# Five kinds of small instruction of the last layers on VectorE in place of GpSimd, with another tie seed

## The chip, the cores and the metric

The kernel runs on one core of a Trainium2 chip. Its engines work side by side, each through its own instruction stream in order: TensorE (PE in the profile; PEld is its weight load), VectorE (DVE), ScalarE (ACT), GpSimd (POOL) and SyncE (SP, which issues nearly all DMAs). An instruction waits for semaphores that other engines raise, and whatever stands behind it on its engine waits with it. The metric is the device time of one execution in microseconds, lower is better. Before the change it is 1130.74 us (median of three runs, 1130.67 to 1131.31).

## The reference: what is computed

The input x is 32 sequences of 64 tokens with 256 features, and a context of the same shape goes with it. Four layers run one after the other, all in float32:

```
x = L0(x, ctx)   # cross attention, 8 heads of 64, over the feature axis; residual
x = L1(x, ctx)   # cross attention, 16 heads of 16; keys and values from LayerNorm(ctx);
                 # x + tanh(gate) * out
x = L2(ctx, x)   # x as latents: attention of x over [ctx, x], RMSNorm, MLP 256-1024-256 with gelu,
                 # plus x
x = L3(x, ctx)   # h = x + selfattention(LayerNorm(x)); h = h + crossattention(LayerNorm(h), ctx);
                 # h + MLP(LayerNorm(h)), 256-1024-256 with gelu
```

In L3 the scores are `scores * mask - 10000 * (1 - mask)` before the softmax. LayerNorm is `(x - mean) * rsqrt(var + 1e-5) * scale + bias`; the kernel folds its scale into the rows of the weight matrix that follows, and its bias into that product's bias.

## The kernel before

Tokens are handled in 8 groups of 256 (two tiles of 128 tokens). Precision comes from splitting: a float32 operand v of a large product is written as a rounded high part hi and a low part v - hi, and three products (hi with hi, hi with low, low with hi) are summed in PSUM. So every weight matrix, every token matrix that is projected and every attention output needs a rounded copy (on ACT) and a subtraction (on VectorE or GpSimd).

L0 is written straight into the engines' streams, in the order of the code, with the first weights' preparation filled in between. It runs to about 459 us. Its instructions carry line 156 in the profile.

L1 to L3 make one plan. The work is cut into 80 attention sets: 16 for L1 (sets 0 to 15), 32 for L2 (16 to 47), 16 for L3's self attention (48 to 63) and 16 for its cross attention (64 to 79). A set covers 128 tokens and all heads (half the heads in L2). Its chain is: scores on PE into the PSUM tile s; in L3 a product with the mask on VectorE (`E<-s,m` for self attention, `E<-s,mk` for cross attention) and an addition on GpSimd (`E<-E,c` or `E<-E,ck`); maximum on VectorE (`mx`); subtraction on VectorE (in L1 and L2 straight from PSUM, `E<-s,mx`), in L3 in every other set on GpSimd (`E<-E,mx` in both cases); Exp on ACT; sum and reciprocal on VectorE (`sm`); in L1 and L2 the scaling by the reciprocals on GpSimd (`E<-E,sm`); transposes on PE, copied by ACT (`PTe`); product with the values on PE. In L3 the output is scaled in place of E (`rb`, VectorE). It is split into `xTho` (ACT) and `xTlo` (a subtraction, in L1 and L2 on VectorE from PSUM, in L3 on GpSimd); `a_fin`, lines 1089 to 1105, does this. There are three E tiles and one tile s, so two to three sets are under way at once.

Around the sets lie "steps": for each group the norm, the split of the context, the projections to keys, values and queries, the output projection and the MLP. Each has a due time, counted in sets. A norm (`norm_steps`, line 1197) has three steps. `ln_stats` (line 888) takes mean and variance with bn_stats and bn_aggr on VectorE, and its factor through `rsqrt` (line 750): epsilon is added (tile `rsq`), then GpSimd raises the result to the power -0.5 (`rstda`; `rstdm` for the norm before the MLP). `ln_apply` (line 899) makes minus mean times factor (`nmra`, `nmrm`), and ACT normalises with the two as bias and scale. `turn` transposes. Its parameter `load` is true for the norms of L1 alone, whose input is the loaded context; there are 16 norms of L3's attentions and 8 before its MLP. `ctx_steps` (line 1229) loads and splits the context for L2 and L3 (`xTh`, `xTl`). `load_unit` (line 503) loads a weight, multiplies its rows by the norm's scale where there is one (tile `wraw`, or `boot` where a spare buffer takes its place) and splits it. In the planned part the 8 such weights are those of L3: keys, values and queries of the self attention, the queries of the cross attention, and the four parts of the first MLP matrix.

The plan then decides the order. `Plan.cost` gives each instruction a duration by engine, form and width, and `Plan.order` is a list scheduler: again and again it takes, among the engines' ready instructions, the one that can start first, and where several can, the one with the smallest due time. To each due time a random number between 0 and TIE sets is added, drawn from SEED. The engine of an instruction and its modelled cost thus decide where it and all others stand, and the seed does as well. What comes out is written into the five streams; on the chip each stream runs in exactly that order, waiting where it must. All planned instructions carry line 125 in the profile, so they are told apart by their tiles. SyncE's DMAs are in the plan, too.

```python
getattr(self.engines[o.key], o.method)(*[real(x) for x in o.p], **{k: real(x) for k, x in o.k.items()})   # 125
at.urgent = at.due + ties.uniform(0, self.TIE) - (3.0 if ... else 0.0)
t, at = min(((t, at) for t, at in cand if t <= t0), key=lambda x: (x[1].urgent, x[1].index))
```

Of the kernel before, what the change touches and what calls it, by code (L numbers as in the profile page):

```python
# [93 lines left out]
class Plan:  # L94
# [2 lines left out]


    RING = {"pj": 40}
    SEED, TIE = 4, 0.5  # L100

    def __init__(self, engines):
        self.engines = engines
# [305 lines left out]
def mk_kernel(ctx: ExitStack, tc: tile.TileContext, a: dict, out: bass.AP):  # L409
# [93 lines left out]
    def load_unit(w, key, slot, ap, rows=None, mul=None, biases=(), then=None):  # L503

        cur["rawn"] += 1
        if cur["raws"] == 2 or cur["rawn"] % 2:
            raw = plan.tile(wraw, "r", [P, 2, D], F32, "wraw", nm("wraw"), 2)
        else:
            raw = wraws[cur["rawn"] // 2 % (cur["raws"] - 2)]
        SY.dma_start(raw, ap.rearrange("(k p) n -> p k n", p=P))  # L510
        yield
        for fn in biases:
            fn(raw)
        t = plan.tile(wpool if slot < NW else cur["w"], "ww", [P, 2, 2, D], F32R, f"w{slot}", nm("w"), 1)
        if rows is not None:
            for k in range(2):
                G.tensor_scalar(raw[:, k], raw[:, k], rows[:, k:k + 1], None, ALU.mult)
        elif mul is not None:
            G.tensor_scalar(raw, raw, mul, None, ALU.mult)
        A.copy(t[:, 0], raw)  # L520
        (V if slot < 4 and plan.on else G).tensor_tensor(t[:, 1], raw, f32(t[:, 0]), ALU.subtract)
        w[key] = (t[:, 0], t[:, 1])
        if then:
            then()
        yield
# [221 lines left out]
            SY.dma_start(m3[i * 64:(i + 1) * 64], a["mask3"])  # L747
        V.tensor_scalar(c3, m3, -1.0, 10000.0, ALU.add, ALU.mult)

    def rsqrt(dst, var, n, eps):  # L750
        t = plan.tile(small, "s", [P, n], F32, "rsq", nm("rsq"), 3)
        G.tensor_scalar(t, var, eps, None, ALU.add)
        G.tensor_tensor(dst, t, nhalf[:, 0:n], ALU.pow)


# [129 lines left out]
            return lambda: V.scalar_tensor_tensor(x1, av[:, 0:D], cst0, s["xt"], ALU.add, ALU.add)  # L885


    def ln_stats(x, tag):

        st = wt([P, 2, 6], F32, "st" + tag, 2)  # L890
        mv = wt([P, 2, 2], F32, "mv" + tag, 2)
        for i in range(2):
            V.bn_stats(st[:, i], x[:, i])
            V.bn_aggr(mv[:, i], st[:, i])
        rstd = wt([P, 2], F32, "rstd" + tag, 2)
        rsqrt(rstd, mv[:, :, 1], 2, 1e-5)
        return mv, rstd

    def ln_apply(x, mv, rstd, tag):
        z = wt([P, 2, D], F32, "z", 2)  # L900
        nmr = wt([P, 2], F32, "nmr" + tag, 2)
        for i in range(2):
            G.tensor_scalar(nmr[:, i:i + 1], mv[:, i, 0:1], rstd[:, i:i + 1], -1.0, ALU.mult, ALU.mult)
            A.activation(z[:, i], x[:, i], AF.Identity, bias=nmr[:, i:i + 1], scale=rstd[:, i:i + 1])
        return z

# [182 lines left out]
    def a_fin(u):  # L1089
        st, i = u["st"], u["i"]  # L1090
        if i == 0 and u["s"] == 0:
            st["o"] = fm_tiles("o")
        o_ = u["at"]
        c = slice(u["s"], u["s"] + 1) if u["two"] else slice(0, 2)
        hv, lv = [t[:, c, i * P:(i + 1) * P] for t in st["o"]]
        ov = o_[:, 0:D].rearrange("p (c t) -> p c t", c=2)[:, c]
        if u["kind"] == "k":
            A.copy(hv, ov)
            V.tensor_tensor(lv, ov, f32(hv), ALU.subtract)
        else:  # L1100
            rb = wt([P, 2, P], F32, "rb", 2)
            A.copy(rb.rearrange("p c t -> p (c t)"), o_[:, D:2 * D])
            V.tensor_tensor(rb, ov, rb, ALU.mult)
            A.copy(hv, rb)
            G.tensor_tensor(lv, rb, f32(hv), ALU.subtract)

    def out_add(w, x, resid, dst):

# [88 lines left out]
    def norm_steps(l, g, key, load, due, src=()):  # L1197

        st = grp.setdefault((l, g), {})
        n = f"{key}{l}{g}"  # L1200

        def fetch():
            st["raw"] = wt([P, 2, D], F32, "craw", 1)
            SY.dma_start(st["raw"], ctok[g])
        x = (lambda: st["raw"]) if load else (lambda: xs[g])
        if load:
            step(n + "a", due - 3, fetch, *src)

        def stats():
            st["ln"] = ln_stats(x(), key)  # L1210

        def apply():
            st["z"] = ln_apply(x(), *st["ln"], key)

        def turn():
            st[key] = to_fm(st["z"], rg if rg == "n" else "")
        rg = "n" if key == "m" else "x"
        step(n + "b", due - 2, stats, *((n + "a",) if load else src))
        step(n + "c", due - 1, apply, n + "b")
        step(n, due, turn, n + "c")  # L1220
# [8 lines left out]
    def ctx_steps(l, g, due, src=()):  # L1229
        st = grp[l, g]  # L1230
        n = f"c{l}{g}"

        def fetch():
            st["raw"] = wt([P, 2, D], F32, "craw", 1)
            SY.dma_start(st["raw"], a["ctxT"][:, g * D:(g + 1) * D].rearrange("(k p) t -> p k t", p=P))

        def split_():
            hi, lo = fm_tiles()
            A.copy(hi, st["raw"])
            G.tensor_tensor(lo, st["raw"], f32(hi), ALU.subtract)  # L1240
            st["c"] = (hi, lo)
        step(n + "a", due - 2, fetch, *src)
        step(n, due, split_, n + "a")
# [431 lines left out]
```

## Time and profile before

| | us |
|---|---|
| median of three runs | 1130.74 |
| profiled execution, its own time | 1132.07 |
| its span, first to last instruction | 1130.3 |
| PE busy | 1067.8 (94%) |
| VectorE busy | 894.9 (79%) |
| ACT busy | 906.3 (80%) |
| GpSimd busy | 761.8 (67%) |
| planned part, about | 459 to 1130 |
| sets 48 to 79 (L3's attentions) begin on VectorE | 785.9 to 1056 |

The times of stretches come from one profiled execution, 1.33 us over the median. A row of a group of instructions names the engine, the operation, the tiles written and read, the shapes and the count, then the busy time, the mean duration, and the idle time of the engine just before such instructions with what ended it. Matmul ends are modelled and matmuls overlap, so a busy PE can have room. The 40 digits of a slice view stand for 28.3 us each.

The rows of the instructions that the change touches, as the whole profile groups them (those with `boot` as output and a scale as second input are the row scales in the spare buffer):

```
L125 POOL TENSOR_TENSOR xTlo<-rb,xTho 128x256 fp32r<-128x256 f32 x32 | 29.0, 906
L125 POOL TENSOR_TENSOR xTl<-boot,xTh 128x512 fp32r<-128x512 f32 x16 | 22.4, 1403
L125 POOL TENSOR_SCALAR wraw<-wraw,vecs 128x256 f32<-128x256 f32 x18 | 16.5, 925
L125 POOL TENSOR_SCALAR nmra<-mva,rstda 128x1 f32<-128x1 f32 x48 | 12.5, 272
```

They hold L1's and L2's instructions as well, which stay where they are.

### The profile page before, as it was taken

To read this page: it belongs to the slowest core of one execution; us is meant where nothing else is said; L and a number is where in the kernel's file an instruction comes from. 1 tells how busy PE (TensorE), PEld (TensorE's weight loads), DVE (VectorE), ACT (ScalarE), POOL (GpSimd) and SP (SyncE) were. 2 spreads that over 40 slices of the span, in tenths; PEclk is the share of its full clock that TensorE was granted. 3 is DMA by queue.
4 is the path that set the end of the run, shared out by engine and by line. 5 is a ranking of instruction groups with operands and counts; after the bars stand their busy time and mean duration, and the time that the engine had idled before them with its cause. 6 is when DMAs were issued, how large, how long until landed. Compare 5 with 4: busy or idle time off the path is not lost.

```text
span 1130.3 us, 35569 instructions
## 1 busy us (share of the span) xinstructions
PE 1067.8 (94%) x14396; PEld 872.2 (77%) x14396; DVE 894.9 (79%) x1575; ACT 906.3 (80%) x2326; POOL 761.8 (67%) x829
## 2 busy tenths in 40 slices
PE   6999999999999999899999999999999988889998
PEld 4666666666666666788898989998988877779998
DVE  4889989897888777688888878777878878777842
ACT  2888888887888789577778889889898777888974
POOL 3788888886778667635546634477866989996520
PEclk9999999999999999899999999999999989989999
DMA  3001211111110100311211100000000111110000
GB/s 96 21 25 36 61 35 49 35 34 44 34 34 25 34 16 2 93 37 58 68 47 47 34 26 26 21 29 22 21 20 21 49 51 51 43 34 21 11 20 29
DMA packets 41300, 41.21 MB, mean 36 GB/s; under 512 B 7059, under 2 KB 37796, under 8 KB 41136
## 3 DMA queue, kind: packets, MB, share of 16 engines
q1 hardware_dynamic: 40816, 38.54, 10.9%
q8 instruction: 114, 1.87, 0.7%
q10 hardware_dynamic: 320, 0.40, 0.1%
q14 instruction: 50, 0.41, 0.1%
HBM read 26.30 MB, written 2.10 MB: 25 GB/s over the span
## 4 chain that ended last, share of the span: by engine, by line
PE 59%; DVE 15%; ACT 10%; POOL 10%; issue 4%; DMA 0%; SPq 0%; DVEq 0%; POOLq 0%; ACTq 0%
PE pj L125 39%; PE pt L156 6%; ACT E L156 5%; PE av L156 5%; PE sc L156 4%; PE s L125 4%; DVE mx L156 3%; POOL E L125 3%; DVE E L125 2%; DVE PT L156 2%; ACT PT L156 2%; DVE sB L156 2%; POOL E L156 2%; DVE mx L125 2%; PE pt L125 1%
## 5 line engine op out<-in xcount | busy, mean ns | idle before, releaser
L156 POOL TENSOR_TENSOR E<-E,rs 128x512 f32<-128x512 f32 x256 | 263.5, 1040 | 84.0 <-DVE rs L156 64.5
L156 ACT ACTIVATE E<-sc,mx 128x256 f32<-128x256 f32 x512 | 238.4, 481 | 23.2 <-DVE rs L156 21.9
L156 DVE TENSOR_REDUCE mx<-sc 128x4 f32<-128x1024 f32 x128 | 155.8, 1217 | 2.8 <-PE sc L156 1.4
L156 PE MATMUL sc<-cd,T 64*128 64x256 f32 x1024 | 144.0, 400 | 10.5 <-ACT E L156 10.0
L125 POOL TENSOR_TENSOR E<-E,sm 128x512 f32<-128x512 f32 x96 | 101.1, 1078 | 68.9 <-DVE sm L125 56.1
L156 PE MATMUL av<-PT,us 128*64 128x256 f32 x1024 | 125.0, 385 | 0.0
L156 PEld LDWEIGHTS pt<-ident,E 64*128 64x128 f32 x2048 | 83.6, 139 | 43.6 <-POOL E L156 15.8
L156 PEld LDWEIGHTS av<-PT,us 128*64 128x64 f32 x1024 | 68.3, 136 | 54.7 <-issue 20.4
L156 PEld LDWEIGHTS sc<-cd,T 64*128 64x128 f32 x1024 | 89.6, 189 | 25.8 <-ACT E L156 17.8
L125 DVE TENSOR_REDUCE sm<-E 128x16 f32<-128x1024 f32 (+1 forms) x80 | 96.0, 1200 | 15.3 <-ACT E L125 15.3
L156 ACT ACTIVATION_READ_ACCUMULATOR E<-sc,mx 128x1 f32 x512 | 108.0, 211 | 0.0
L156 PE MATMUL pt<-ident,E 64*128 64x64 f32 x2048 | 98.2, 228 | 6.1 <-ACT PT L156 2.2
L125 ACT COPY PTe<-pj 128x512 f32<-128x512 f32 x160 | 88.0, 590 | 19.2 <-PE pj L125 17.1
L125 PE MATMUL pj<-ident,E 128*128 128x128 f32 x640 | 90.8, 281 | 8.0 <-DVE rb L125 2.5
L156 ACT COPY PT<-pt 128x512 f32<-128x512 f32 x128 | 75.6, 591 | 24.3 <-PE pt L156 22.8
L125 PE MATMUL pj<-w,xThh 128*128 128x256 f32 x512 | 93.4, 287 | 0.1
L125 PE MATMUL pj<-xThn,w 128*128 128x256 f32 x512 | 92.2, 285 | 0.7 <-DVE rb L125 0.4
L156 DVE COPY PT<-pt 128x512 f32<-128x512 f32 x128 | 86.0, 672 | 5.2 <-PE pt L156 5.1
L125 ACT ACTIVATE E<-E 128x1024 f32<-128x1024 f32 x80 | 84.9, 1062 | 5.8 <-DVE E L125 4.6
L125 PEld LDWEIGHTS pj<-ident,E 128*128 128x128 f32 x640 | 71.6, 143 | 16.7 <-issue 3.6
L125 DVE TENSOR_TENSOR xTlh<-u,xThh 128x512 fp32r<-128x512 f32 x64 | 54.8, 861 | 29.9 <-ACT xThh L125 29.5
L156 DVE RECIPROCAL rs<-sm 128x2 f32<-128x2 f32 x256 | 40.1, 156 | 46.5 <-ACT E L156 43.7
(223 smaller groups left out, 2798.3 us busy)
## 6 DMA issues: line engine op xcount, KB each, us to landing
kb<-kfm SPq DMA_DIRECT2D x44, 128.0 KB
xd<-in_x SPq DMA_DIRECT2D x32, 128.0 KB
cd<-in_ctx SPq DMA_DIRECT2D x32, 128.0 KB
boot<-in_ctxT SPq DMA_DIRECT2D x16, 256.0 KB
kb<-kfm SPq DMA_DIRECT2D x64, 64.0 KB
xt<-in_x SPq DMA_DIRECT2D x16, 128.0 KB
boot<-in_ctx SPq DMA_DIRECT2D x8, 256.0 KB
out<-x SPq DMA_DIRECT2D x8, 256.0 KB
```

The lines of the kernel that those rows point to most:

```text
L125: getattr(self.engines[o.key], o.method)(*[real(x) for x in o.p], **{k: real(x) for k, x in o.k.items()})
L156: return f(*p, **k)
```

## The change

In L3 five kinds of instruction go to VectorE: the addition of epsilon in the norms, minus mean times factor (one instruction for the pair of tiles in place of two), the row scales of the weights that the plan loads, the low part of the context (L3 alone, `l == 3`), and the low part of the attention output where the tile index i is 0, every other set. The power stays on GpSimd. The seed of the ties goes from 4 to 9; with that, and with the other engines and costs, the scheduler puts the whole planned part into a new order. L0 and the first weights are as before.

```diff
@@ -97,7 +97,7 @@
 
 
     RING = {"pj": 40}
-    SEED, TIE = 4, 0.5
+    SEED, TIE = 9, 0.5
 
     def __init__(self, engines):
         self.engines = engines
@@ -514,7 +514,7 @@
         t = plan.tile(wpool if slot < NW else cur["w"], "ww", [P, 2, 2, D], F32R, f"w{slot}", nm("w"), 1)
         if rows is not None:
             for k in range(2):
-                G.tensor_scalar(raw[:, k], raw[:, k], rows[:, k:k + 1], None, ALU.mult)
+                (V if plan.on else G).tensor_scalar(raw[:, k], raw[:, k], rows[:, k:k + 1], None, ALU.mult)
         elif mul is not None:
             G.tensor_scalar(raw, raw, mul, None, ALU.mult)
         A.copy(t[:, 0], raw)
@@ -747,9 +747,9 @@
             SY.dma_start(m3[i * 64:(i + 1) * 64], a["mask3"])
         V.tensor_scalar(c3, m3, -1.0, 10000.0, ALU.add, ALU.mult)
 
-    def rsqrt(dst, var, n, eps):
+    def rsqrt(dst, var, n, eps, late=False):
         t = plan.tile(small, "s", [P, n], F32, "rsq", nm("rsq"), 3)
-        G.tensor_scalar(t, var, eps, None, ALU.add)
+        (V if late else G).tensor_scalar(t, var, eps, None, ALU.add)
         G.tensor_tensor(dst, t, nhalf[:, 0:n], ALU.pow)
 
 
@@ -885,7 +885,7 @@
             return lambda: V.scalar_tensor_tensor(x1, av[:, 0:D], cst0, s["xt"], ALU.add, ALU.add)
 
 
-    def ln_stats(x, tag):
+    def ln_stats(x, tag, late):
 
         st = wt([P, 2, 6], F32, "st" + tag, 2)
         mv = wt([P, 2, 2], F32, "mv" + tag, 2)
@@ -893,14 +893,17 @@
             V.bn_stats(st[:, i], x[:, i])
             V.bn_aggr(mv[:, i], st[:, i])
         rstd = wt([P, 2], F32, "rstd" + tag, 2)
-        rsqrt(rstd, mv[:, :, 1], 2, 1e-5)
+        rsqrt(rstd, mv[:, :, 1], 2, 1e-5, late)
         return mv, rstd
 
-    def ln_apply(x, mv, rstd, tag):
+    def ln_apply(x, mv, rstd, tag, late):
         z = wt([P, 2, D], F32, "z", 2)
         nmr = wt([P, 2], F32, "nmr" + tag, 2)
+        if late:
+            V.scalar_tensor_tensor(nmr, mv[:, :, 0], -1.0, rstd, ALU.mult, ALU.mult)
         for i in range(2):
-            G.tensor_scalar(nmr[:, i:i + 1], mv[:, i, 0:1], rstd[:, i:i + 1], -1.0, ALU.mult, ALU.mult)
+            if not late:
+                G.tensor_scalar(nmr[:, i:i + 1], mv[:, i, 0:1], rstd[:, i:i + 1], -1.0, ALU.mult, ALU.mult)
             A.activation(z[:, i], x[:, i], AF.Identity, bias=nmr[:, i:i + 1], scale=rstd[:, i:i + 1])
         return z
 
@@ -1102,7 +1105,7 @@
             A.copy(rb.rearrange("p c t -> p (c t)"), o_[:, D:2 * D])
             V.tensor_tensor(rb, ov, rb, ALU.mult)
             A.copy(hv, rb)
-            G.tensor_tensor(lv, rb, f32(hv), ALU.subtract)
+            (G if i else V).tensor_tensor(lv, rb, f32(hv), ALU.subtract)
 
     def out_add(w, x, resid, dst):
 
@@ -1207,10 +1210,10 @@
             step(n + "a", due - 3, fetch, *src)
 
         def stats():
-            st["ln"] = ln_stats(x(), key)
+            st["ln"] = ln_stats(x(), key, not load)
 
         def apply():
-            st["z"] = ln_apply(x(), *st["ln"], key)
+            st["z"] = ln_apply(x(), *st["ln"], key, not load)
 
         def turn():
             st[key] = to_fm(st["z"], rg if rg == "n" else "")
@@ -1237,7 +1240,7 @@
         def split_():
             hi, lo = fm_tiles()
             A.copy(hi, st["raw"])
-            G.tensor_tensor(lo, st["raw"], f32(hi), ALU.subtract)
+            (V if l == 3 else G).tensor_tensor(lo, st["raw"], f32(hi), ALU.subtract)
             st["c"] = (hi, lo)
         step(n + "a", due - 2, fetch, *src)
         step(n, due, split_, n + "a")
```

## The prediction

> **What bounds the kernel now.** I read the page's slices first, to see where the limit changes; then busy time by stretch, cut where the last part's attention sets begin; then the groups, waits and timeline inside the tight stretch.
>
> ```profile
> PE   6999999999999999899999999999999988889998
> POOL 3788888886778667635546634477866989996520
> PEclk9999999999999999899999999999999989989999
> ```
>
> TensorE (PE) is full nearly everywhere, except in slices 33 to 36 of 40 (about 904 to 1017 us), where GpSimd (POOL) shows nines and the granted clock dips twice. The next view cuts 858 to 1130 us where VectorE (DVE) takes up sets 56, 60, 64, 68, 72, 76 and where the last set, 79, has begun (sets 48 to 79 are the last part's).
>
> ```profile
> core 0: us, PE busy (x) PEld busy (x) DVE busy (x) ACT busy (x) POOL busy (x), PEclk, DMA share, GB/s
> 858.00:883.90 25.90, 24.09 (x405) 21.04 (x403) 21.98 (x33) 22.06 (x45) 18.66 (x15) 1.00 0.06 21
> 883.90:916.60 32.70, 30.90 (x427) 27.62 (x426) 24.99 (x47) 21.73 (x48) 29.65 (x28) 0.84 0.16 51
> 916.60:949.30 32.70, 27.35 (x418) 24.05 (x418) 28.81 (x47) 26.77 (x57) 31.82 (x31) 0.95 0.20 61
> 949.30:976.90 27.60, 24.36 (x380) 21.41 (x379) 23.85 (x37) 23.39 (x50) 26.60 (x27) 1.00 0.11 36
> 976.90:1030.20 53.30, 47.66 (x606) 43.73 (x607) 37.67 (x52) 44.66 (x90) 48.93 (x53) 0.94 0.11 34
> 1030.20:1056.00 25.80, 25.80 (x350) 24.30 (x350) 21.83 (x32) 22.84 (x42) 15.71 (x12) 1.00 0.04 13
> ```
>
> From 883.9 to 1030.2 (146.3 us, sets 60 to 75) GpSimd is busy 137.0 us, 94%, and VectorE 115.3, 79%. PE's busy share there flatters it: back to back, a 128x256 matmul starts 0.119 us after the last one, a 128x128 transpose 0.109, a set's 16 score groups take 0.70 (gaps and lengths in PE's records), and by these prices sets 60 to 75 hold only 95.6 us of matmuls and 11.2 of scores: PE has some 40 us to spare. GpSimd sets the pace, and the waits of this stretch agree (total, times, longest):
>
> ```profile
> DVE mx L125 <- POOL E L125: 8.3, 5, 2.9
> PE pj L125 <- POOL xTl L125: 4.5, 3, 2.2
> ```
>
> The first line: VectorE's maximum waits for GpSimd's mask addition; the second: PE waits for the context's low part, one of the moved instructions.
>
> **The change, part by part.** Five kinds of instruction leave GpSimd.
>
> - Epsilon added to the variance (rsq): 23 seen, 7.1 us.
> - Minus mean times factor (nmr): 46 of [128,1], 13.6 us; on VectorE one of [128,2] for a pair.
> - Row scales of 8 weights (wraw, boot): 16 of 128x256, 15.8 us.
> - The context's low part (xTl): 8 of 128x512, 11.7 us.
> - The output's low part (xTlo), every other set: 16 at 0.906, 14.5 us.
>
> Together 63 us. In the tight stretch the rows sum to 38 us: rsq 3.6, nmr 7.1, scales 8.3, xTl 11.7, half of xTlo 7.5. GpSimd falls from 137 to about 100 of 146 us and no longer sets the pace.
>
> What VectorE takes on. In the new program's order, 51 moved instructions lie between set 60 and set 76. Undisturbed prices come from the nearest VectorE rows: bias adds of one column, 0.15 us, for 12 rsq and 12 nmr (3.7); the row `boot<-boot,rrms` at its shortest, 0.34, for 10 scales (3.4); xTlh, same shape and same two SBUF inputs, 0.68, for 8 xTl (5.4); 0.41 for 9 xTlo (3.7; the 128x256 product rb took 0.41). Sum 16.2. The order also brings 3.0 us of other VectorE work here (two more sums, one more subtraction, two xTlh fewer). Less 3.6, since consecutive instructions overlap by about 0.07 us in the timeline.
>
> The unknown is what these instructions lose to GpSimd. These three rows show it (start, duration; the first is VectorE's, the others GpSimd's):
>
> ```profile
> 886.50 0.67 DVE L125 TENSOR_SCALAR bq3c<-bq3c 128x2 f32<-128x2 f32 x1
> ```
> ```profile
> 884.78 2.36 POOL L125 TENSOR_TENSOR E<-E,c 128x1024 f32<-128x1024 f32 x1
> 887.10 1.29 POOL L125 TENSOR_TENSOR xTl<-boot,xTh 128x512 fp32r<-128x512 f32 x1
> ```
>
> Two columns take 0.67 us instead of 0.15, until GpSimd's addition ends at 887.1. VectorE's subtraction with both inputs in SBUF shows the same:
>
> ```profile
> L125 DVE TENSOR_TENSOR E<-E,mx x16: 1162/1786/3450, 793.1 to 1058.3; 128x1024 f32<-128x1024 f32 x16
> L125 DVE TENSOR_TENSOR xTlh<-u,xThh x22: 660/692/2456, 788.5 to 1055.1; 128x512 fp32r<-128x512 f32 x22
> ```
>
> (ns, least/median/most.) The first loses 0.73 us on average, the second 0.39 (mean 1.06). In the tightest part, 883.9 to 976.9, eleven such instructions lost 4.0 us, 0.37 each, with GpSimd 95% busy. At 68% that is 0.27. Some of it costs nothing, because VectorE's next maximum waits for that very addition (the 8.3 us above); I take 0.20. The bounds are 0 (median of the second row) and 0.5 (mean over all 47 such rows from 785 to 1060, the slowest stretch for them).
>
> The Trainium skill (GPSIMD Engine Reference, section Key points) speaks against the change: it names contention with VectorE instructions that have two SBUF inputs or run in a two-port mode, which by form takes in nearly all the moved ones. If each waited half a mean GpSimd instruction whenever one ran, I estimate 0.4 us each and a time near 1140; the second row's median of 0.69 says that many don't wait.
>
> **Sum for sets 60 to 75.** VectorE's 115.3 us hold 10 of such losses (4.0 to set 71, 6 after). Without them 105.3, plus 16.2 + 3.0 - 3.6 = 121. The new order has 70 exposed instructions here (20 before): 14 us at 0.20.
>
> New waits come with the move. nmr now stands on VectorE and waits for GpSimd's power (0.71 us); behind it queue the sets' maxima and sums, for which ACT's exponentials and then PE's transposes wait. The nearest row, the second layer's scaling `boot<-boot,rrms` behind the same power, idled 0.35 us a result: for 12 results 0 to 4 us, and I take 2, since GpSimd will have room. The power in turn waits for VectorE's rsq; behind it on GpSimd stand mask additions, and the 46 us that GpSimd gains hide that (without them, 0.7 us each, 8 us). xTl and xTlo wait on VectorE for ACT's rounded copy, as xTlh does (6.4 us of idling for 22, 0.29 each): for 17 of them 0 to 5 us.
>
> That last and all other idling of VectorE I put at 4%: it was 98 and 99% busy in its fullest 10 us (860 to 870, 940 to 950), and 88% from 916.6 to 949.3, where GpSimd was full too; I stay nearer the first because the engine that VectorE waited for gets room. (121 + 14 + 2) x 1.04 = 142.4, against 146.3: **-3.9**. At 12% idling it would be 153.
>
> Sets 48 to 59, 98.0 us. PE needs 27.2, 38.6 and 20.3 us for the three groups of four (VectorE's 22.0 is longer in the third). The new order holds 27.5, 31.6 and 26.3: the longer engine's sum falls from 87.8 to 85.4, and of the 10.2 us above it about 2 go with the uneven third group (25.9 against 22.0): **-4.4**. VectorE is at 31 in the middle group, so this is tight.
>
> Set 76 to the end, 100.1 us. PE alone: between the scores of 76 and 79 the new order holds 31.2 us of matmuls instead of 22.8, after them 61.6 instead of 67.5: +8.4 - 5.9, **+2.5**. This stretch is the same work put elsewhere, and gives nothing.
>
> Before set 48 the changed tie seed reorders everything, but PE's matmuls sum to 269 us in both orders, and PE is busy 317 of 327 us: 0, with bounds of -4 (half the 9.7 us idle) and +4. Table loads on ACT stay (23 runs of Gelu in both orders). SyncE's queue carries the same DMAs in another order, at 13% of the engines' time or less: 0; were a key block late, the wait at PE would be the 2.2 us of the xTl line.
>
> Sum -5.8. The profiled execution took 1132.07 us (span 1130.3 and 1.8 around it), 1.33 above the median of 1130.74: 1126.3 for it, **1125** as a median.
>
> **Rivals.**
>
> 1. *VectorE becomes the bound, slower.* Place: sets 60 to 75. The rest of my sum is -1.9. At 0.37 us a loss (as now) these sets take (123 + 26) x 1.04 = 155, +8.7, in all 1137; at 0.5 they take 164, in all 1147. It decides from 0.28 us a loss: (123 + 70 x 0.28) x 1.04 = 148.3 eats the other gains. For it: 51 short instructions on the engine that every set visits four or five times. Against: GpSimd is a quarter less busy.
> 2. *The whole stall goes.* No losses: 123 x 1.04 = 128, -18.4, in all 1110. For it: PE's spare 40 us, and the granted clock (0.84, 0.95 and 0.94 in three of the rows, 10 us of PE's time) coming back. Against: VectorE would be 96% busy.
> 3. *Nothing to measure.* GpSimd's relief and VectorE's load cancel within 2 us: 1131. For it: my sum is the difference of two large figures. Against: only that the two would have to meet within 2 us.
>
> **How the numbers follow.** Forecast (1116 to 1128) 0.39; rival 2 and what lies between (below 1116) 0.15; no change 0.08; rival 1, with the first sets' +4 in it, 0.38. Differences within 0.2% (2.3 us) can't be told from none here. Faster 0.54, same 0.08, slower 0.38. Range: from the no-loss bound, 1109, to the 0.5 bound, 1147; about 1 in 10 lies on each side.
>
> **What the changed profile would show.** GpSimd at two thirds between sets 60 and 76, its nines gone; VectorE at 95% there; moved rows on VectorE with means of 0.35 (rsq), 0.55 (scales), 0.9 (xTl) and 0.6 us (xTlo); no PE wait on `POOL xTl`; the stretch near 142 us and set 76 to the end near 102. Means twice those, or the maxima waiting behind nmr, would show rival 1. I am wrong if losses to GpSimd exceed 0.28 us each, or if sets 0 to 47 take more than 331 us.

## The result, and the profile after

The change makes the kernel slower: the median is 1155.23 us (1153.8 to 1156.72, four runs) against 1131.03 (1130.67 to 1131.73, four runs) for the kernel before, a ratio of 1.0214 with a 95% interval of 1.0201 to 1.0227. The prediction said 1125, between 1109 and 1147. The profiled execution has a span of 1152.9 us, 22.6 more than before.

The page after, its busy times, three rows of slices, and the chain that ended last by engine:

```profile
PE 1070.8 (93%) x14396; PEld 873.1 (76%) x14396; DVE 948.2 (82%) x1663; ACT 906.8 (79%) x2326; POOL 705.5 (61%) x717
DVE  3889989997898776887898887887989889998752
POOL 2688888876787667554464444456855667664410
PEclk9999999999999999999999999999998989899999
PE 56%; DVE 23%; ACT 12%; issue 4%; POOL 4%; DMA 1%; SPq 0%; DVEq 0%; POOLq 0%; ACTq 0%
```

GpSimd's nines are gone from slices 34 to 36, as forecast, and it lost 56 us over the whole span. VectorE gained 53 us, and shows nines in these three slices now. In the chain VectorE has 23% (15% before) and GpSimd 4% (10% before). The granted clock dips as it did before: 0.92 over sets 60 to 75, 0.93 before.

Busy time by stretch, cut where VectorE takes up sets 60, 64, 68, 72, 76, and in the last row the four together (sets 60 to 75):

```profile
886.80:922.50 35.70, 31.50 (x426) 27.62 (x427) 30.10 (x57) 23.43 (x49) 22.46 (x14) 0.86 0.12 38
922.50:960.10 37.60, 28.79 (x415) 25.08 (x415) 33.58 (x50) 25.48 (x54) 25.00 (x19) 0.91 0.19 57
960.10:994.70 34.60, 25.22 (x394) 21.63 (x392) 33.35 (x49) 23.00 (x48) 22.99 (x17) 0.90 0.10 32
994.70:1048.40 53.70, 47.20 (x603) 42.45 (x604) 49.56 (x82) 47.07 (x94) 33.64 (x27) 0.97 0.10 34
886.80:1048.40 161.60, 132.71 (x1833) 116.79 (x1834) 146.60 (x234) 118.98 (x245) 104.10 (x76) 0.92 0.13 40
```

The columns are the window and its length, then busy time of PE, PE's weight loads, VectorE, ACT and GpSimd, and the granted clock. Sets 60 to 75 take 161.6 us where they took 146.3. VectorE is busy 146.6 of them (91%; before 79%), GpSimd 104.1 (64%; before 94%). By busy time the pace has gone from GpSimd to VectorE, and VectorE's own busy time is already as long as the whole stretch was before.

The waits inside this stretch (total us, times, longest):

```profile
POOL E L125 <- DVE E L125: 20.0, 7, 7.8
PE pj L125 <- DVE xTl L125: 8.7, 2, 4.6
POOL rstda L125 <- DVE rsq L125: 7.9, 3, 5.5
POOL rstdm L125 <- DVE rsq L125: 6.4, 3, 2.5
POOL E L125 <- DVE mx L125: 5.9, 5, 3.5
```

Both lines shown of before are gone: VectorE's maximum no longer waits for GpSimd's mask addition, and PE no longer waits for GpSimd's low part. In their place GpSimd waits for VectorE, and PE waits for the same low part, which now stands in VectorE's queue: 8.7 us in two waits, against 4.5 in three.

VectorE's groups in the stretch (busy us, mean ns, idle time before them):

```profile
L125 DVE TENSOR_TENSOR E<-E,mx 128x1024 f32<-128x1024 f32 x9 | 14.8, 1640 | 0.1
L125 DVE TENSOR_TENSOR xTl<-boot,xTh 128x512 fp32r<-128x512 f32 x8 | 10.0, 1254 | 0.0
L125 DVE TENSOR_SCALAR rsq<-mva 128x2 f32<-128x2 f32 x8 | 7.1, 886 | 0.2
L125 DVE SCALAR_TENSOR_TENSOR nmra<-mva,rstda 128x2 f32<-128x2 f32 x8 | 3.6, 447 | 0.0
L125 DVE TENSOR_SCALAR boot<-boot,vecs 128x256 f32<-128x256 f32 x4 | 2.7, 725 | 0.0
```

Adding epsilon to two columns (`rsq<-mva`, the norms before the attentions) takes 0.89 us on average, five times the 0.17 that it takes undisturbed; the low part 1.25 where 0.68 is undisturbed. The idle time before them is nothing: what these instructions lose, they lose while they count as busy. One of them, VectorE's rows first and GpSimd's second (start, duration):

```profile
991.06 0.18 DVE L125 BATCH_NORM_AGGREGATE mva<-sta 128x2 f32<-128x6 f32 x1
991.27 1.94 DVE L125 TENSOR_SCALAR rsq<-mva 128x2 f32<-128x2 f32 x1
993.12 0.24 DVE L125 RECIPROCAL sm<-sm 128x16 f32<-128x16 f32 x1
```
```profile
990.83 2.35 POOL L125 TENSOR_TENSOR E<-E,ck 128x1024 f32<-128x1024 f32 x1 [4.63 <-DVE E L125]
993.29 0.70 POOL L125 TENSOR_TENSOR rstda<-rsq,nhalf 128x2 f32<-128x2 f32 x1
```

GpSimd's mask addition ends at 993.18 and VectorE's two columns at 993.21. In between VectorE stands, and the power that needs the result could not have started on GpSimd either.

Counted over the whole stretch: 70 of VectorE's instructions are of an exposed kind, that is, of the kinds that were seen to lose time while GpSimd is busy: those with two inputs in SBUF, and additions of a constant or scalings of two or more columns within SBUF. Together they took 26.8 us more than they take undisturbed, 0.38 each. Three instructions of rare forms left out, 27 of 67 began while GpSimd ran an instruction with two full inputs, and these hold 25.7 us of it. The others lost nothing to speak of, also when GpSimd ran an instruction with one input or the short power.

### The profile page after: what moved, and what is told of

It reads as the page before. It is cut to its first block, busy times and chain, and to the rows that moved or that the text cites. A ratio compares the mean times of both kernels' runs of the same rounds, so it can differ in the third digit from the quotient of the medians.

```text
span 1152.9 us, 35545 instructions
## 1 busy us (share of the span) xinstructions
PE 1070.8 (93%) x14396; PEld 873.1 (76%) x14396; DVE 948.2 (82%) x1663; ACT 906.8 (79%) x2326; POOL 705.5 (61%) x717
## 4 chain that ended last, share of the span: by engine, by line
PE 56%; DVE 23%; ACT 12%; issue 4%; POOL 4%; DMA 1%; SPq 0%; DVEq 0%; POOLq 0%; ACTq 0%
PE pj L125 36%; PE pt L156 7%; ACT E L156 5%; PE av L156 5%; PE sc L156 4%; PE s L125 4%; DVE mx L156 3%; DVE E L125 3%; DVE mx L125 2%; DVE sm L125 2%; DVE PT L156 2%; ACT PT L156 2%; DVE sB L156 2%; POOL E L156 1%; PE pt L125 1%
## 5 line engine op out<-in xcount | busy, mean ns | idle before, releaser
L156 PE MATMUL sc<-cd,T 64*128 64x256 f32 x1024 | 144.7, 402 | 10.2 <-ACT E L156 9.5
L156 PE MATMUL av<-PT,us 128*64 128x256 f32 x1024 | 125.0, 385 | 0.0
L125 DVE TENSOR_TENSOR xTlh<-u,xThh 128x512 fp32r<-128x512 f32 x64 | 63.4, 994 | 27.2 <-ACT xThh L125 27.1
```

The costliest lines, as they stand in the source:

```text
L156: return f(*p, **k)
```

## The experiments

"Sets 60 to 75" is the same stretch in every kernel, cut by the start of set 60 and of set 76 on VectorE. "Losses" are the time over undisturbed durations of the exposed instructions, counted as above; in brackets is how many there were, with the one-column forms of the small kinds counted in. A kernel with the old order keeps every engine's sequence as in the kernel before: the planner goes on treating the moved instruction as GpSimd's, and only where it is written out does it go to VectorE. New orders move work between stretches, so for those the whole time counts more than the one stretch.

The expectations name theories by letters. V: VectorE pays for the moves; O: the new order costs the time. P: VectorE's own time and its losses to GpSimd; C: the added crossings between the engines. R and S: the order is poor because the moved instructions stand too late, or because the planner's prices are too low; G: any order planned with VectorE so full is poor; N: the seeds were unlucky. Others are explained where they stand.

| kernel | median us | ratio to before, 95% | sets 60 to 75 | VectorE busy | GpSimd busy | losses (exposed) |
|---|---|---|---|---|---|---|
| before | 1131.03 | | 146.3 | 115.3 | 137.0 | 10.1 (20) |
| after | 1155.23 | 1.0214 (1.0201 to 1.0227) | 161.6 | 146.6 | 104.1 | 26.8 (70) |
| old_order_moved | 1140.43 | 1.0087 (1.0072 to 1.0102) | 151.4 | 137.6 | 103.4 | 20.8 (80) |
| new_order_back | 1166.25 | 1.0310 (1.0293 to 1.0328) | 170.0 | 120.5 | 139.8 | 10.9 (19) |
| old_order_small | 1129.08 | 0.9983 (0.9973 to 0.9992) | 141.7 | 125.0 | 128.7 | 16.5 (56) |
| old_order_low | 1135.98 | 1.0043 (1.0027 to 1.0060) | 148.2 | 133.9 | 124.8 | 21.8 (36) |
| old_order_scales | 1133.93 | 1.0024 (1.0013 to 1.0035) | 145.0 | 117.5 | 130.2 | 10.2 (28) |
| new_order_narrow | 1151.09 | 1.0165 (1.0147 to 1.0182) | 159.5 | 142.0 | 103.6 | 19.3 (94) |
| old_order_small_ck | 1128.71 | 0.9974 (0.9962 to 0.9985) | 140.0 | 124.1 | 125.0 | 15.8 (56) |
| old_order_narrow | 1126.48 | 0.9964 (0.9951 to 0.9976) | 139.7 | 122.1 | 124.7 | 13.1 (68) |
| old_order_wide | 1130.04 | 0.9990 (0.9981 to 0.9999) | 141.1 | 123.9 | 124.6 | 17.3 (44) |

### Places or order: four kernels

The change does two things at once. It moves instructions, and the planner draws another order (seed 9 in place of 4, and the moved instructions at their new prices). Two kernels take the seeds apart: the kernel before with the new seed, and the change with the old one.

```diff
-    SEED, TIE = 4, 0.5
+    SEED, TIE = 9, 0.5      # s9_old_places: this alone; s4_new_places: all but this
```

> The kernel before with nothing but the tie seed at 9 (no instruction moved). Theory V (VectorE pays for the moved instructions: their own time and what they lose while GpSimd reads two inputs; the order matters by a few us): 1124 to 1138 us. Theory O (the new order is what costs the 24 us): about 1155 us.

Measured: 1134.81 us, ratio 1.0035 (1.0022 to 1.0049). By its trace sets 0 to 47 took 332.8 us (before 326.9), and from set 48 to the end it took 340.4, 4 us less than before: what this draw lost, it lost ahead of the last layer.

> The kernel after with the tie seed back at 4 (all moves kept, the planner orders anew). Theory V: 1148 to 1162 us, sets 60 to 75 near 160 us on VectorE and VectorE above 88% busy there. Theory O: near 1131 us.

Measured: 1166.18 us, ratio 1.0315 (1.0300 to 1.0331). So seed 9 is not what costs the time: with the old places it is only 0.35% slower, and with the new places it is the better of the two seeds. The second kernel came out 4 us above V's range.

The next two keep an order and change only the engine that an instruction is written to (minus mean times factor as two one-column instructions in the old order, since it has two places there):

```diff
-        getattr(self.engines[o.key], o.method)(...)
+        getattr(self.engines[o.run], o.method)(...)
-    def engine(self, key):
+    def engine(self, key, run=None):
+                    o.run = run or key
+    M = plan.engine("G", "V")        # planned as GpSimd's, written to VectorE
-                G.tensor_scalar(raw[:, k], raw[:, k], rows[:, k:k + 1], None, ALU.mult)
+                (M if plan.on else G).tensor_scalar(raw[:, k], raw[:, k], rows[:, k:k + 1], None, ALU.mult)
...                                   # the other four kinds likewise
```

> The order of the kernel before is kept in every stream (the planner still takes the moved instructions for GpSimd's), but they run on VectorE: the moves alone, no new order. Theory V: 1145 to 1165 us, sets 60 to 75 at 158 to 165 us instead of 146, the exposed instructions there losing about 0.37 us each. Theory O: 1120 to 1131 us, since GpSimd is relieved and nothing is reordered.

Measured: 1140.43 us. Its stretch, and the largest wait in it:

```profile
885.00:1036.40 151.40, 132.77 (x1821) 118.68 (x1821) 137.62 (x239) 116.77 (x242) 103.44 (x76) 0.91 0.13 43
```
```profile
POOL rstda L125 <- DVE rsq L125: 22.0, 7, 4.3
```

Even with nothing else touched, the moves cost 9.3 us (1140.4 against 1131.2 in the same series). That lies between the ranges of V and O. VectorE is busy 91% of the stretch, and GpSimd stands 22 us waiting for the additions of epsilon that it used to do itself.

The reverse keeps the order of the change and gives the moved instructions back to GpSimd:

```diff
+    M = plan.engine("V", "G")        # planned as VectorE's, written to GpSimd
-        (V if late else G).tensor_scalar(t, var, eps, None, ALU.add)
+        (M if late else G).tensor_scalar(t, var, eps, None, ALU.add)
...                                   # the other four kinds likewise
```

> The order of the kernel after is kept in every stream, but the moved instructions run on GpSimd again (minus mean times factor as two instructions): the new order alone, no moves. Theory V: 1130 to 1146 us, VectorE below 82% in sets 60 to 75, GpSimd the pace there again. Theory O: 1155 us or more.

Measured: 1166.25 us. The waits of its tight stretch:

```profile
PE pj L130 <- POOL xTl L130: 13.3, 5, 5.4
ACT boot L130 <- POOL nmra L128: 13.0, 5, 4.6
```

In the order that was planned for the new places, the moves gain 11 us (1166.3 to 1155.2). In the order planned for the old places they cost 9. The order costs more than the moves: 1155.2 against 1140.4, with the same instructions on the same engines save for the form of one. So V and O both hold in part: 9 us and 15 by this path, moves first. By the other, order first, the order costs 35 us and the moves give 11 back, so an order and the places that it was planned for belong together, and the split is no property of either alone.

The table says a little of where the order's share lies. new_order_narrow, which is told further down, keeps the order of the change and loses about as much to GpSimd as old_order_moved (19.3 and 20.8 us), and its stretch is still 8.1 us longer: 4.4 us of it VectorE's busy time, 3.7 its idling. So the order's cost there is not the losses.

### Each group of moves alone, in the old order

The same edit for one group each: epsilon and minus mean times factor (small), the low parts of context and outputs (low), the row scales (scales).

```diff
+        (M if late else G).tensor_scalar(t, var, eps, None, ALU.add)                     # small
+            (M if late else G).tensor_scalar(nmr[:, i:i + 1], mv[:, i, 0:1], rstd[:, i:i + 1], -1.0, ALU.mult, ALU.mult)
+            (G if i else M).tensor_tensor(lv, rb, f32(hv), ALU.subtract)                 # low
+            (M if l == 3 else G).tensor_tensor(lo, st["raw"], f32(hi), ALU.subtract)
+                (M if plan.on else G).tensor_scalar(raw[:, k], raw[:, k], rows[:, k:k + 1], None, ALU.mult)   # scales
```

> The order of the kernel before in every stream; only the addition of epsilon and minus mean times factor run on VectorE (the latter as two one-column instructions). Theory P (port: what costs is the instruction's own time on VectorE plus what it loses to GpSimd; these two lost nothing when all moves were run in the old order, 0.16 and 0.20 us each): 60 to 75 within 3 us of 146, in all 1129 to 1134 us. Theory C (crossings: the extra hand-over from GpSimd's power to VectorE and back is what costs): 1137 to 1141 us, most of the 9.3 us of all moves.

> The order of the kernel before; only the context's low part and every other output's low part run on VectorE. Theory P: the dearest of the moves on VectorE (17 instructions near 0.97 us in sets 60 to 75, 16 us on VectorE against 18 off GpSimd): 1134 to 1141 us. Theory C: 1128 to 1133 us.

> The order of the kernel before; only the weights' row scales run on VectorE (10 in sets 60 to 75, 0.34 to 0.5 us each there against 0.93 to 1.17 on GpSimd). Theory P: 4 to 5 us more on VectorE, 8 to 10 off GpSimd, which sets the pace: 1125 to 1131 us. Theory C: 1131 us, no hand-over is added on a norm's path.

Measured against 1131.3 in the same series: small 1129.08, a gain of 2.2; low 1135.98, a loss of 4.7; scales 1133.93, a loss of 2.6. Together 5.1 of the 9.3 us; the other 4.2 come only when all are moved. The low parts take VectorE's busy time in the stretch from 115 to 134 us and fill it to 90%, and the stretch gets longer although GpSimd gives up 12 us. The small ones free 8 us on GpSimd for 10 on VectorE and shorten the stretch by 4.6 us. They are the group with the most crossings, VectorE to GpSimd and back for each norm, and the only one that gains: that speaks for P and against C. The scales shorten the stretch by 1.3 us and the time still grows by 2.6, which neither P nor C expected. The profiled execution, at 1132.37, is the fastest of nine, so the stretches do not settle where that goes.

### What makes the new order dear: three attempts

The moved instructions could stand too far back in VectorE's queue. The planner gives a head start of three sets to instructions of VectorE and ACT that read PSUM; here the moved ones get it too.

```diff
-            at.urgent = at.due + ties.uniform(0, self.TIE) - (3.0 if at.key in "VA" and ...
+            at.urgent = at.due + ties.uniform(0, self.TIE) - (3.0 if at.ops[0].rush or at.key in "VA" and ...
```

> The kernel after, but the planner gives the moved instructions the same head start of three sets that it gives to instructions emptying PSUM. Theory R (the new order is bad because on a full VectorE the moved instructions are planned behind every PSUM read that is ready, so norms and projections come late): 1135 to 1145 us, sets 60 to 75 below 155 us. Theory S (the new order is bad because the planner prices VectorE's small instructions at 0.2 us and they take 0.3 to 0.9): 1150 to 1165 us, as without the head start.

Measured: 1159.82 us, ratio 1.0255 (1.0230 to 1.0280). No gain; if anything 4.6 us worse.

Or the planner's prices for VectorE could be too low, since it knows of no losses. Here short instructions on SBUF cost 0.6 in place of 0.2, and those with two tensors 0.25 more.

```diff
-                return 0.2, 0.05, None
+                return (0.6 if o.method in ("tensor_scalar", "scalar_tensor_tensor") and not out_of_banks else 0.2), 0.05, None
-            return 0.3 + w * (...
+            return (0.55 if o.method == "tensor_tensor" else 0.3) + w * (...
```

> The kernel after, but the planner prices VectorE's small SBUF instructions at 0.6 us instead of 0.2 and its SBUF subtractions 0.25 us higher, near the measured means, and orders anew. Theory S (the new order is bad because these prices are too low): 1132 to 1146 us. Rival G (a greedy order with VectorE this full is poor whatever the prices): 1150 to 1168 us.

Measured: 1156.06 us, ratio 1.0215 (1.0197 to 1.0233), no different from the change. Sets 60 to 75 shrank to 151.5 us, but with fewer of PE's matmuls in them (1702 against 1833); the stretches before and after took up what they gave. And a third seed with the new places:

```diff
-    SEED, TIE = 9, 0.5
+    SEED, TIE = 1, 0.5
```

> The kernel after with a third tie seed, 1. Rival G (any order planned with the moved places is poor, seeds 4 and 9 gave 1166 and 1155): 1148 to 1168 us. Rival N (the two seeds were unlucky): 1131 to 1142 us, as the moves in the old order.

Measured: 1170.07 us, ratio 1.0337 (1.0321 to 1.0352). Five orders planned with the new places take 1155 to 1170. So R, S and N fall, as they were tried: neither this head start, nor these prices, nor the seed accounts for it.

The next question was whether every newly drawn order is poor, or only one with VectorE so full. Four kernels were planned anew: nothing moved and seed 1, and one group moved with seed 4, with the engine changed for the planner too.

```diff
-    SEED, TIE = 4, 0.5
+    SEED, TIE = 1, 0.5                                                                   # s1_old_places
+        (V if late else G).tensor_scalar(t, var, eps, None, ALU.add)                     # plan_small
+            V.scalar_tensor_tensor(nmr, mv[:, :, 0], -1.0, rstd, ALU.mult, ALU.mult)
+            (G if i else V).tensor_tensor(lv, rb, f32(hv), ALU.subtract)                 # plan_low
+            (V if l == 3 else G).tensor_tensor(lo, st["raw"], f32(hi), ALU.subtract)
+                (V if plan.on else G).tensor_scalar(raw[:, k], raw[:, k], rows[:, k:k + 1], None, ALU.mult)   # plan_scales
```

> The kernel before, planned anew with SEED 1 (all operations at their old places). Open: the five orders that were planned with the moved places take 1155 to 1170, the two planned with the old places 1131 and 1135. Theory G (an order planned with VectorE this full is poor, whatever the ties): the old places leave room, 1128 to 1138. Rival K (every new draw of the order is poor; seeds 4 and 9 of the old places were lucky): 1145 to 1165.

> The kernel before with SEED 4, only epsilon and minus mean times factor moved, and the order planned anew with them at their new place. In the old order this move gave 1129.1. G: it adds least to VectorE, so the new plan costs little: 1128 to 1138, VectorE below 0.87 of sets 60 to 75. K: a new draw like any other, 1145 to 1165.

> The kernel before with SEED 4, only the context's low part and half of the outputs' low parts moved, order planned anew. In the old order this move gave 1136.0, with VectorE at 0.90 of sets 60 to 75. G: here the planner's VectorE is full, so most of the 15 to 25 us of a new plan comes with this move: 1150 to 1165, sets 60 to 75 at 160 or more. K: 1145 to 1165 as for the others. If neither, and below 1140: it takes all three moves together.

> The kernel before with SEED 4, only the weights' row scales moved, order planned anew. In the old order this move gave 1133.9. G: VectorE gets 0.81 of sets 60 to 75, little more than before: 1130 to 1140. K: 1145 to 1165.

| planned anew with | median us of each order | the same moves in the old order |
|---|---|---|
| nothing moved | 1134.8 (seed 9), 1139.4 (seed 1) | 1131 |
| small | 1139.3 | 1129.1 |
| scales | 1139.9 | 1133.9 |
| low | 1144.9 | 1136.0 |
| all | 1155.2 (seed 9), 1156.1 (prices), 1159.8 (head start), 1166.2 (seed 4), 1170.1 (seed 1) | 1140.4 |

Neither theory holds as it was put: only plan_scales came out within a range of G, and none within K's. A new draw costs something even with nothing moved: 3.7 and 9.2 us against the kernel before in their series, whose order is the best of the three. With one group moved it costs 6 to 10 us, and the gain that the small moves bring in the old order is lost in it. With all moved it costs 15 to 30. So the price is highest with everything moved, but between the groups it does not follow VectorE's load: the small moves, which load VectorE less, pay 10.2 us and the low parts 8.9. What in the planner's choice makes it so is still open.

### The form: one column or two

The losses depend on how an instruction is written. In old_order_moved minus mean times factor, as one-column instructions, never lost anything, and in the change, as one instruction over two columns, it did. This kernel keeps the order of the change and writes both small kinds as two one-column instructions:

```diff
+        if getattr(o, "narrow", False):
+            dst, one, *rest = [real(x) for x in o.p]
+            for i in range(2):
+                ...tensor_scalar(dst[:, i:i + 1], one[:, i:i + 1], ...)
+            return
```

> The kernel after with its order in every stream, but the addition of epsilon and minus mean times factor are each two one-column instructions on VectorE (24 more instructions in sets 60 to 75). Theory P (losses to GpSimd set VectorE's pace; one-column forms with a pointer never lost in 48 cases, while the 128x2 forms lost 9 us in sets 60 to 75 of the kernel after): those losses go, 2 to 3 us of plain time come on top, sets 60 to 75 at 152 to 158 us instead of 162, in all 1145 to 1152 us. Rival L (more instructions on a full VectorE only cost): 1156 to 1161 us.

Measured: 1151.09 us, ratio 1.0165 (1.0147 to 1.0182), some 4 us less than the change, as P expected. Its rows in the last layers:

```profile
L129 DVE TENSOR_SCALAR rsq<-mva x26: 94/144/155, 787.1 to 1015.6; 128x1 f32<-128x1 f32 x26
L131 DVE TENSOR_SCALAR nmra<-mva,rstda x26: 121/203/212, 790.4 to 1019.4; 128x1 f32<-128x1 f32 x26
```

(Least, median, most in ns.) Not one took longer than 0.22 us, where the two-column ones took up to 2.3. The losses in the stretch fall from 26.8 to 19.3 us; the stretch itself falls only from 161.6 to 159.5, and P had expected 158 at most.

One more kernel takes the gaining group, in the old order, and relieves GpSimd a little further: the constant for the cross mask goes to ACT.

```diff
-            G.tensor_scalar(u["ck"], u["mk"], -1.0, 10000.0, ALU.add, ALU.mult)
+            A.activation(u["ck"], u["mk"], AF.Copy, scale=10000.0, bias=-10000.0)
```

> The order of the kernel before; epsilon and minus mean times factor on VectorE as before, and the cross attention's mask constant (12 of 128x64 in sets 60 to 75, 4.4 us on GpSimd) on ACT, which is 80% busy there. If GpSimd's queue still sets part of the pace with the small ones gone (it is 91% busy there): 1123 to 1128 us; if VectorE does by now: 1128 to 1130 us.

Measured: 1128.71 us, ratio 0.9974 (0.9962 to 0.9985): faster than before, and not to be told from old_order_small, as expected if VectorE sets the pace there by now. Its rows:

```profile
L128 DVE TENSOR_SCALAR rsq<-mva x13: 154/157/2340, 789.3 to 995.0; 128x2 f32<-128x2 f32 x13
L128 DVE TENSOR_SCALAR nmra<-mva,rstda x26: 125/203/214, 794.9 to 998.3; 128x1 f32<-128x1 f32 x26
```

The two-column additions lose, the one-column rows do not. From it the form was tried once in each direction, with nothing else changed: epsilon in one-column form (narrow), and minus mean times factor in two-column form (wide).

```diff
+            for i in range(2):                                                           # old_order_narrow
+                self.engines["V"].tensor_scalar(dst[:, i:i + 1], one[:, i:i + 1], *rest)
+                self.engines["V"].scalar_tensor_tensor(real(dst), real(mean), -1.0, real(rstd), ALU.mult, ALU.mult)   # old_order_wide
```

> old_order_small_ck (1128.7) with each addition of epsilon written as two one-column instructions, same order. In that run 7 of 21 additions over two columns began while GpSimd ran an instruction with two inputs, and took 0.6 to 2.3 us instead of 0.16. Theory W (an instruction of one column with a pointer or a constant does not lose to GpSimd, one of two columns waits for the end of the GpSimd instruction): every rsq row at 0.13 to 0.2, none above; some 5 us of VectorE's time gone; 1125 to 1128.5. Rival H (where the one-column ones lost nothing, they happened to come at a good moment): about a third of the first ones of a pair again take over 0.5 us, and the time is 1128 to 1131.

> old_order_small_ck (1128.7) with minus mean times factor as one instruction of two columns for a pair, as the change writes it, in place of two of one column, same order. W: those that begin while GpSimd runs an instruction with two inputs (16 of 42 of the one-column ones did, without loss) now wait for its end, rows of 0.5 to 2.3 us in 6 to 9 of 21; 1130 to 1135. H: means of 0.15 us, fewer instructions, 1126 to 1129.

Measured: narrow 1126.48 us, ratio 0.9964 (0.9951 to 0.9976); wide 1130.04, ratio 0.9990 (0.9981 to 0.9999). First the rows of narrow, then those of wide:

```profile
L131 DVE TENSOR_SCALAR rsq<-mva x26: 134/142/153, 786.2 to 989.6; 128x1 f32<-128x1 f32 x26
L131 DVE TENSOR_SCALAR rsq<-mvm x16: 119/143/154, 959.3 to 1083.8; 128x1 f32<-128x1 f32 x16
L133 DVE TENSOR_SCALAR nmra<-mva,rstda x26: 122/202/216, 790.3 to 992.9; 128x1 f32<-128x1 f32 x26
```
```profile
L133 DVE TENSOR_SCALAR rsq<-mva x13: 152/159/2340, 789.6 to 995.6; 128x2 f32<-128x2 f32 x13
L131 DVE SCALAR_TENSOR_TENSOR nmra<-mva,rstda x13: 145/151/1227, 795.2 to 998.8; 128x2 f32<-128x2 f32 x13
L131 DVE SCALAR_TENSOR_TENSOR nmrm<-mvm,rstdm x8: 144/161/1857, 967.6 to 1091.5; 128x2 f32<-128x2 f32 x8
```

In narrow, 30 of the 84 one-column instructions began while GpSimd ran an instruction with two full inputs, and none took over 0.22 us. In wide, 13 of 42 two-column ones did, and they averaged 0.6 to 1.1 us, by kind. It is the form that decides, not the moment. For epsilon only the width differs; for minus mean times factor the operation differs as well, since the two-column form reads both inputs as tensors and the one-column form takes one as a per-row scalar. The order of the three medians (1126.5, 1128.7, 1130.0) is the one expected, though neighbouring intervals overlap. Narrow is the fastest kernel of this study, 4.5 us below the one before in its series.

## Why the prediction was wrong

The terms of the sum, and what the trace after shows:

| stretch | predicted change | measured change |
|---|---|---|
| start to set 0 | 0 | +2.0 (459.0 to 461.0) |
| sets 0 to 47 | 0 | -0.6 (326.9 to 326.3) |
| sets 48 to 59 | -4.4 | +1.4 (98.0 to 99.4) |
| sets 60 to 75 | -3.9 | +15.3 (146.3 to 161.6) |
| set 76 to the end | +2.5 | +4.3 (100.2 to 104.5) |

**What was right.** GpSimd was the fullest engine of the tight stretch, and falls to two thirds; its wait lines go. That it alone set the pace is less sure: 7 and 8 us taken off it in the old order (scales, small) shortened the stretch by only 1.3 and 4.6. Without losses VectorE's work in sets 60 to 75 was put at 121 us and is 119.8. Sets 0 to 47 were put at no change and changed by -0.6, but with some luck: the same seed with nothing moved took 5.9 us more there, outside the stated bounds of 4.

**The step that failed: "14 us at 0.20".** The 70 exposed instructions were there, but they lost 26.8 us, 0.38 each. The moved rows show it: 1.25 us for xTl where 0.9 was forecast, 0.89 for most of rsq where 0.35 was. The rows of before gave this price: the 20 exposed instructions of the same stretch lost 10 us, 0.50 each, and the eleven of its tightest part 0.37. The prediction took the smaller, scaled it by GpSimd's busy time to 0.27, and then cut it to 0.20 on the ground that some of it costs nothing. That last cut could hold at most while VectorE would have waited for GpSimd anyway; on the engine that sets the pace a loss has nothing to hide behind. The scaling was also off. What holds VectorE is GpSimd's instructions with two full inputs, and these fell only from 106 to 89 us, 73% to 55% of the stretch, since the small ones and the scales that left were not among them. By that share, 0.50 x 55 / 73 gives 0.38, the measured value; that it fits so closely is partly luck, since old_order_low lost 0.60 each at 60% and s9_old_places 0.40 at 76%. By VectorE's account this term is 12.8 of the 19.2 us by which the stretch was missed. That is an account, not a test: new_order_narrow, in the order of the change, lost 7.5 us less to GpSimd, and its stretch shortened by 2.1.

**The second: idling "at 4%".** VectorE idled 15.0 of 161.6 us, 9.3%. With 4% of 137 us and the 2 us for the power the prediction had 7.5; the difference, 7.5 us, and -1.2 from the work itself make up the rest. In every kernel here whose VectorE carries the low parts in sets 60 to 75, it is busy 85 to 92% of them, and never near the 96% that the prediction borrowed from its fullest 10 us. The 88% that it had seen over 33 us was the better guide.

**The third: "-4.4" for sets 48 to 59.** It followed from the longer engine's sum per group of four sets, with VectorE "tight" in the middle. VectorE went from 79 to 89 us busy there, and the stretch lasts 99.4. The two other terms, +2.0 at the start and +1.8 more than predicted at the end, complete the sum. The start's code is the same in both kernels, and its time ranged from 459.0 to 462.1 us over all of these kernels, so that term is hardly the change's doing.

**Rival 1** named what happened: VectorE becomes the bound in sets 60 to 75, and it decides from 0.28 us a loss. At the measured 0.37 to 0.38 it gave only 1137, because it kept the 4% of idling and the gain in sets 48 to 59. The range's upper end, 1147, assumed losses of 0.5 and was passed with 0.38: its bounds varied the losses and left the other terms as they were. Rival 2 fell: VectorE never came near 96%. Rival 3 fell too.

**What the prediction did not separate** is the move from the order. It costed the new order's instructions by their sums per stretch, which say nothing on how they interleave. By the runs, 9 of the 24 us are the moves in an unchanged order, and 15 come with the newly drawn order. How much of these any new draw would have cost can't be read off: with nothing moved, seed 9 made the part from set 48 on 4 us shorter than before and seed 1 made it 5 us longer, and it is in this part that the change loses. What in the order makes the 15 us stays open.

**The rule that spoke against the change** was priced in the prediction at 0.4 us an instruction and a time near 1140, and set aside for a row's median. The measured 0.38 sides with its price; the time is 15 us above. The runs also bear out another page of the Trainium skill, in part. SBUF — State Buffer, section Who interferes with whom, says that whichever of VectorE and GpSimd issues first gets a shared pair of ports for the whole instruction and the other blocks fully, where VectorE's instruction has two SBUF inputs and GpSimd's reads SBUF, or where VectorE's runs in a two-port mode. The row at 991.27 shows such a block, 1.94 us to within 0.03 us of the end of GpSimd's addition. On GpSimd's side the runs are narrower than the page: its instructions with one input, which read SBUF too, held up none of the exposed ones by more than 0.25 us. VectorE: DVE Perf Modes, section What auto-detection actually checks, ties the two-port mode of an instruction with one source to operands in SBUF whose outermost non-unit dimensions are both even, or equal. An operand of one column has nothing to split, which would fit the 84 one-column rows without a loss; the runs show that the form decides, and not that the mode is why.

## What to carry to other kernels

Before moving short work from GpSimd to VectorE, price each moved instruction by its form. Where it can wait for GpSimd, a rough price is the undisturbed time plus the share of the time in which GpSimd runs instructions with two full inputs, times what is left of one, and it is safest counted in full where VectorE sets the pace; one-column forms went free of that here, and the small moves, partly or wholly in that form, were the only ones that gained. Where a planner writes the order, compare in a fixed order first: here a new draw alone moved the time by 3.7 and 9.2 us, about as much as the best kernel gained (4.5) or more.

## What the runs showed that was not expected

- One column against two: the addition of a constant to 128x1 took 0.09 to 0.16 us in each of 84 cases (42 each in new_order_narrow and old_order_narrow) and lost nothing behind a running GpSimd instruction. The same addition to 128x2 took 0.12 to 2.34, so two narrow instructions (0.28 us) are cheaper than one wide one where GpSimd is busy.
- Not all of GpSimd's instructions hold VectorE. In the tight stretch of the change, seven exposed ones began during an instruction with one input or a power over two columns, and lost 0.1 us together; the 27 that began during one with two full inputs lost 25.7. In the last layer of all the kernels here, 85 exposed ones of two or more columns began with over 0.1 us of a one-input GpSimd instruction still to run, and none lost more than 0.25 us.
- A GpSimd that waits can't hold VectorE up. In old_order_moved the additions of epsilon took 0.16 us each in sets 60 to 75, although over two columns, because GpSimd stood waiting for them (22 us in seven waits); what they did not lose, GpSimd idled. The old order alone does not bring this: in old_order_small_ck, also in the old order, 7 of 21 such additions began during a GpSimd instruction with two full inputs, at up to 2.34 us.
